# A four-layer graph kernel on one core: layer 1 takes the newest quarter last, mixing puts weighing beside scores, elu is written back into PSUM

## The chip, the cores and the metric

The kernel runs on one core of one Trainium2 chip. The core has five engines that run their own instruction streams and meet by semaphores: TensorE (PE in the profile), VectorE (DVE), ScalarE (ACT), GpSimd (POOL) and SyncE (SP, used here to issue DMAs). TensorE reads its operands from SBUF and writes into PSUM; the others read and write both, GpSimd only SBUF here. The metric is device time in microseconds of one execution, the median of several runs.

## The reference

Four layers, each a layer norm over `x + layer(x)`, with x of shape (8, 2048, 64) and one adjacency matrix of 2048 x 2048. What matters here are layers 0 and 1:

```python
h = x @ W
alpha = softmax(where(H.T > 0, leaky_relu(h @ a_node), NEG))    # per hyperedge e
agg = einsum('ben,bnf->bef', alpha, h)
beta = sigmoid((h @ a_gn)[:, None, :] + (agg @ a_ge)[:, :, None])
all_he = elu(beta[..., None] * h[:, None] + (1 - beta[..., None]) * agg[:, :, None])
industry = einsum('nm,bmf->bnf', adj / deg, x @ W_ind)
coefs1 = softmax(where(H > 0, attn_scores(elu(agg)), NEG))      # attn_scores(f) = tanh(f @ fcW) @ av
g = einsum('bne,benf->bnf', coefs1, all_he)
coefs2 = softmax(attn_scores(stack([industry, g])))             # the mixing: two candidates
out0 = coefs2[0] * industry + coefs2[1] * g
x = layernorm(x + out0)                                         # layer 0
x = layernorm(x + (D^-1/2 (adj + I) D^-1/2) @ x @ W1.T)         # layer 1
```

Layers 2 (a Chebyshev graph convolution with an attention matrix) and 3 (three propagation steps) follow, and the change does not touch them.

## The kernel before

The batch of 8 is taken as four pairs (p = 0 to 3), so that two batches of 64 features fill 128 columns. The 2048 nodes are 16 tiles of 128 (t), or four quarters of 512 (c). The adjacency matrix stays in SBUF. Matmul operands are split by `split` (L167, L168) into a high part, cast on ScalarE, and a low part, so that every product with the adjacency takes two matmuls.

**One stream of filler.** Layer 0's products `adj @ x` (`products`, L383 to L418) and layer 1's (`layer1`, L1012) are a generator. It yields after each matmul, and other stages take from it by `fill(n)` (L420): n matmuls with the adjacency are written between two steps of their own, so TensorE has work while the other engines do theirs. Each matmul also counts a `tick` (L309 to L330): work handed to `after(n, f)` or `later(n, f)` is written n matmuls later. The order of instructions on each engine is thus largely written out in the program; what is wrapped in `tc.keep_in_program_order` (`pin`) keeps its place, and the rest may be moved by a scheduler.

**Hyperedge stage** (`begin`, L746 to L768, and the loop at L774 to L808). A node lies in 1 to 12 hyperedges; nodes are sorted by that count, so the 16 tiles have 12, 5, 5, 4, ... down to 1 slots, 57 in all. Per slot: three matmuls make `pz` in PSUM, eight fills at most are taken; VectorE multiplies `pz` by the ratios `R` (L793), ScalarE takes exp (L795) into `y` in SBUF, VectorE forms elu from both into `y` (L797) and weighs `y` by `co` (L800 for the first slot, L802 for others), and GpSimd adds it to `acc` (L803). After the last slot of a tile an indirect DMA scatters `acc` to `gs_hbm` (L805). `begin` for the next tile is called after the first slot's matmuls: it splits the gathered row `hrow` (low part on GpSimd), makes `ps` and from it, on VectorE, `R` and `co` (L761, L764, L765, L767). `slots` (L281 to L300) transposes the slot numbers into `pslot`, casts them twice on ScalarE (L288) and makes the one-hot matrices of a tile with two ScalarE operations per slot (L299, L300). `pz`, `pslot` and other small tiles share a PSUM pool tag `mm` of three buffers; the fills accumulate in other PSUM tiles. Also in this stage: the degrees of the nodes (`degrees`, L341 to L356) and their inverses (`inverses`, L358 to L381).

**Mixing** (L1050 to L1070), 16 steps i = (pair, quarter). `mix_load` and `mix_g` load the two candidates, `mix_ind` and `mix_g` bring them into one layout (`pi`, `pg`), `mix_scores` (L916 to L926) makes four `pf` matmuls and their tanh, takes differences and adds `gn` to the residual `r`; `mix_weigh` (L935, L937) makes `pd` from the differences, its tanh `th` and from it the weighed candidate `ind`; `mix_end` (L948 to L957) transposes it into `pt`, adds, normalizes (`normalized`, L843 to L867: VectorE, ScalarE's square, GpSimd's power, VectorE) and stores the quarter of x1, after which SP loads the residual of step i + 2. Between the groups, `fill(8)` or `fill(9)`. All these PSUM tiles share a tag `mm` of four buffers.

**Layer 1.** When a quarter of x1 is stored, `l1_parts` (L969, L972) reloads it into one of two staging buffers (`staged`, L204), scales it by `dinv` on GpSimd and splits it. `layer1(p)` runs over two halves g of the columns, and in each over all 16 tiles t (so the quarters 0, 1, 2, 3 in order); then `l1_end` (L991 to L996) multiplies by W1 (`po`), adds `x1` (reloaded by `l1_load`, L981) and normalizes. `load_xn` (L1010) loads the finished 1 MB of a pair on ScalarE's queue.

**End of the mixing.** After the last step the program drains stores by `fill(1)`, loads the node embeddings into `xn` by SP (L1098), takes `fill(32)`, and then for four blocks calls `make_el` (L1107 to L1117; its matmul is `pb`) with `fill(16)` between; after the second, `load_xn` may start. Then the check of the norms, and the remaining fills. Layer 2 begins with `apt_tile` (L1149 to L1156).

Of the kernel before, what the change touches and what calls it, by code (L numbers as in the profile page):

```python
# [56 lines left out]
def tile_gnn_fast(  # L57
# [28 lines left out]
    P = 128  # L86
# [230 lines left out]
    def after(n, f, *more):  # L317

        soon.append([n, lambda: (f(), after(*more) if more else None)])
# [22 lines left out]
    def products():  # L342
# [3 lines left out]
        def degrees(g):  # L346
            du = pph.tile([P, 2, C], F32, tag="ph", name=f"du{g}", bufs=2)
            for t in range(NT):
                for i in range(2):
                    mm(  # L350
                        du[:, i, :], lhsT=ones_r, rhs=adj_c(t, 2 * g + i), start=t == 0, stop=t == NT - 1
                    )
                    yield
            for i in range(2):
                c = 2 * g + i
                r = slice(c * P // NCH, (c + 1) * P // NCH)  # L356
                evacuate(deg4[r, :], du[r, i, :])

        def inverses():

            pdc = places["small"]([P, JT, P], "pdc")
            for j in range(JT):
                transpose(pdc[:, j, :], deg4[:, cols(j, P)])
            pdc = pdc.rearrange("p j (c r) -> p c j r", c=NCH)[:, :, :, 0]
            d1 = deg1.rearrange("p (c j) -> p c j", c=NCH)
            nc.vector.tensor_scalar(d1, pdc, 1.0, None, op0=ALU.add)
            nc.gpsimd.tensor_tensor(dinv, deg1, neg_half[:, :NT], ALU.pow)
            nc.vector.tensor_scalar(d1, pdc, 1.0, None, op0=ALU.max)
            nc.vector.reciprocal(deg1, deg1)
            for _ in range(20):  # L370
                yield
            for c in range(NCH):
                pt = places["small"]([P, C], "pinv")
                for j in range(JT):
                    k = c * JT + j
                    transpose(pt[:, cols(j, P)], deg1[:, k:k + 1].to_broadcast([P, P]))
                row = va.tile([P, C], F32, tag="ut", name="inv", bufs=2)
                nc.scalar.copy(row, pt)
                nc.sync.dma_start(inv_hbm[:, cols(c)], row)
                for _ in range(4):  # L380
                    yield  # L381

        for p in range(NP):  # L383
# [358 lines left out]
    with ExitStack() as pb_scope:  # L742
        pps = pb_scope.enter_context(tc.tile_pool(name="pb_ps", bufs=1, space=PSUM))
        places["small"] = lambda shape, name: pps.tile(shape, F32, tag="mm", name=name, bufs=3)
        pl = pb_scope.enter_context(tc.tile_pool(name="pl", bufs=1))

        def begin(t):

            k = tiles.index(t)
# [11 lines left out]
            nc.vector.tensor_tensor(  # L761
                R[:, 0:S], ps[:, 0:S, 0, :], hrow[:, None, BF:BF + 8].to_broadcast([P, S, B]), ALU.add
            )
            nc.vector.tensor_reduce(R[:, S], ps[:, 0:S, 1, :].rearrange("p s b -> p b s"), AX.X, ALU.add)  # L764
            nc.vector.reciprocal(R[:, 0:S + 1], R[:, 0:S + 1])  # L765
            co = pl.tile([P, 12, B], F32, tag="co", name="co", bufs=2)
            nc.vector.tensor_tensor(  # L767
                co[:, 0:S], ps[:, 0:S, 1, :], R[:, S:S + 1, :].to_broadcast([P, S, B]), ALU.mult  # L768
            )
            return S, both, ohs, R, co  # L770


        tiles = [*range(NT - 2), NT - 1, NT - 2]
        now = begin(0)  # L774
        slots(tiles[1], pps, "mm", 3)
        for k, t in enumerate(tiles):
            S, both, ohs, R, co = now
            acc = pl.tile([P, B, F], F32, tag="acc", name="acc", bufs=2)
            for s in range(S):
                pz = pps.tile([P, C], F32, tag="mm", name="pz", bufs=3)  # L780
# [12 lines left out]
                nc.vector.tensor_tensor(z, z, R[:, s, :, None].to_broadcast([P, B, F]), ALU.mult)  # L793
                y = pl.tile([P, B, F], F32, tag="y", name="y", bufs=3)
                nc.scalar.activation(y, z, AF.Exp, bias=-1.0)  # L795

                nc.vector.scalar_tensor_tensor(y, z, 1.0, y, op0=ALU.max, op1=ALU.min)  # L797
                cb = co[:, s, :, None].to_broadcast([P, B, F])
                if s == 0:
                    nc.vector.tensor_tensor(acc, y, cb, ALU.mult)  # L800
                else:
                    nc.vector.tensor_tensor(y, y, cb, ALU.mult)  # L802
                    nc.gpsimd.tensor_tensor(acc, acc, y, ALU.add)  # L803

            nc.gpsimd.indirect_dma_start(  # L805
                out=gs_hbm[:], out_offset=bass.IndirectOffsetOnAxis(ap=order[:, t:t + 1], axis=0),
                in_=acc.rearrange("p b f -> p (b f)"), in_offset=None,
            )  # L808

    hrp_scope.close()  # L810
    hy_scope.close()
# [94 lines left out]
    def mix_scores(i):  # L906
# [56 lines left out]
    def l1_parts(p, c):  # L963

        if (p, c) not in stored:
            due.add((p, c))
            return
        y = staged("y")
        nc.sync.dma_start(y, x1_hbm[p][:, wide(c), :])  # L969

        def scale():
            pin(nc.gpsimd.tensor_tensor(y, y, dinv[:, wide(c), None].to_broadcast([P, JT, P]), ALU.mult))  # L972

        def cast():
            part[p, c] = split(va, y, f"v{c}", 1, [P, JT, P], pin=True)

        after(16, scale, 6, cast)

    def l1_load(p, c):
        x1 = staged("x1")  # L980
        nc.sync.dma_start(x1, x1_hbm[p][:, wide(c), :])  # L981
        return x1

    def l1_end(p, c, ut, x1):
# [5 lines left out]
        def add_up():  # L990
            pin(nc.vector.tensor_tensor(r, po, dinv[:, wide(c), None].to_broadcast([P, JT, P]), ALU.mult))  # L991
            pin(nc.gpsimd.tensor_tensor(r, r, x1, ALU.add))

        def end():
            if p < NP - 1:
# [2 lines left out]
            load_xn()  # L998

        dst = xn[p][:, wide(c), :] if p == NP - 1 else r  # L1000
        after(4, add_up, 6, *normalized(lp, r, dst, True, end))

    room = []

# [6 lines left out]

    def layer1(p):  # L1012

        for g in range(2):
            own = (2 * g, 2 * g + 1)
            ug = None
            for t in range(NT):
                while (p, t // JT) not in part:
                    yield "wait"
                if ug is None:  # L1020
                    ug = pph.tile([P, 2, C], F32, tag="ph", name="u1", bufs=2)
                    u = {c: ug[:, c % 2, :] for c in own}
                for i in range(2):
                    for c in own:
                        mm(
                            u[c], lhsT=part[p, t // JT][i][:, t % JT, :], rhs=adj_c(t, c),
                            start=t == 0 and i == 0, stop=t == NT - 1 and i == 1,
                        )
                        tick()
                        yield  # L1030
                if g == 1 and p + 1 < NP and t % JT == JT - 1:
                    l1_parts(p + 1, t // JT)
            for k, c in enumerate(own):
                ut = va.tile([P, C], F32, tag="ut", name="ut", bufs=2)
                pin(nc.scalar.copy(ut, u[c]))
# [91 lines left out]
    norms = staged("emb").rearrange("p t f -> p (t f)")[:, 0:NT * D].rearrange("p (t d) -> p t d", d=D)  # L1127
    nc.sync.dma_start(norms, emb.rearrange("(t p) d -> p t d", p=P))
    nc.vector.tensor_tensor(norms, norms, norms, ALU.mult)
    nrm = ap_.tile([P, NT], F32, name="nrm")  # L1130
    nc.vector.tensor_reduce(nrm, norms, AX.X, ALU.add)
    nc.vector.tensor_reduce(wrong[:, 5:6], nrm, AX.X, ALU.max)
    nc.vector.tensor_scalar(wrong[:, 5:6], wrong[:, 5:6], SUM_LIMIT, None, op0=ALU.is_gt)
    for _ in filler:
        pass

# [1486 lines left out]
```

## Time and profile before

| | before |
|---|---|
| runs | 1742.09, 1739.12, 1742.03 us; median 1742.03 |
| profiled execution | 1745.85 us, of which the span is 1743.7 |
| mean granted TensorE clock | 0.984 |
| instructions | 27994 |
| busy in the span: PE, DVE, ACT, POOL | 1660.8 (95%), 832.2 (48%), 589.5 (34%), 571.8 (33%) us |
| hyperedge stage, mixing, end of the mixing | about 63 to 221, 221 to 436, 436 to 523 us |

A group's line in the profile reads: line, engine, operation, output tile <- input tiles, shapes, count, then the busy time in us and the mean of one instruction in ns, and then the idle time of that engine just before the group's instructions with what ended it. A line of the waits reads: engine, what it wanted to do, what it waited for, then us in total, how many times, and the longest. A line of the timeline has the start, the duration, the instruction, and in brackets the engine's idle time before it. In a table by stage, each engine has its busy time and, in brackets, its instructions; PEclk is the granted clock as a share of full speed.

### The profile page before, as it was taken

To read this page: it belongs to the slowest core of one execution; us is meant where nothing else is said; L and a number is where in the kernel's file an instruction comes from. 1 tells how busy PE (TensorE), PEld (TensorE's weight loads), DVE (VectorE), ACT (ScalarE), POOL (GpSimd) and SP (SyncE) were. 2 spreads that over 40 slices of the span, in tenths; PEclk is the share of its full clock that TensorE was granted. 3 is DMA by queue.
4 is the path that set the end of the run, shared out by engine and by line. 5 is a ranking of instruction groups with operands and counts; after the bars stand their busy time and mean duration, and the time that the engine had idled before them with its cause. 6 is when DMAs were issued, how large, how long until landed. Compare 5 with 4: busy or idle time off the path is not lost.

```text
span 1743.7 us, 27994 instructions
## 1 busy us (share of the span) xinstructions
PE 1660.8 (95%) x11196; PEld 1209.8 (69%) x11196; DVE 832.2 (48%) x1547; ACT 589.5 (34%) x1031; POOL 571.8 (33%) x515
## 2 busy tenths in 40 slices
PE   6888899999899999999999999999989999999996
PEld 4667666666674444478788878888767877878775
DVE  7688845778642221210136147777523433433332
ACT  1345533444222212111213267878512222212221
POOL 4578845556534443422023001313210200202001
PEclk9999999999999999999999999999999999999998
DMA  9833334444330000027344457675571121211211
GB/s 342 277 126 124 125 122 136 142 145 146 112 121 6 30 27 5 24 71 293 112 133 138 117 137 154 138 168 123 152 260 43 49 61 43 61 48 42 57 42 39
DMA packets 171180, 195.83 MB, mean 112 GB/s; under 512 B 71536, under 2 KB 116336, under 8 KB 169760
## 3 DMA queue, kind: packets, MB, share of 16 engines
q1 hardware_dynamic: 160096, 154.54, 30.4%
q0 software_dynamic: 8544, 30.68, 5.2%
q10 hardware_dynamic: 2400, 8.72, 1.4%
q8 instruction: 90, 1.47, 0.4%
q14 instruction: 50, 0.41, 0.1%
HBM read 126.72 MB, written 67.17 MB: 111 GB/s over the span
## 4 chain that ended last, share of the span: by engine, by line
PE 78%; DVE 4%; DMA 3%; POOL 2%; issue 2%; ACT 1%; SPq 1%; POOLq 0%; ACTq 0%; DVEq 0%
PE u L172 39%; PE ua L172 13%; PE py L172 8%; PE pw L172 6%; PE ug L172 3%; PE pr L172 2%; PE po L172 1%; PE pf L172 1%; PE pt L175 1%; PE s L172 1%; PE pd L172 1%; PE pi L172 1%; PE pz L172 1%; POOL ln_r L862 0%; DMA adj_more<-adj_hbm 0%
## 5 line engine op out<-in xcount | busy, mean ns | idle before, releaser
L172 PE MATMUL ua<-pt,xn 128*128 128x512 f32 x512 | 230.2, 592 | 1.4 <-DVE pt L1150 1.4
L172 PEld LDWEIGHTS ua<-pt,xn 128*128 128x128 f32 x512 | 96.9, 190 | 111.1 <-issue 104.0
L1514 DVE COPY w_half<-pw 128x512 f32<-128x512 f32 x160 | 109.7, 705 | 91.1 <-PE pw L172 90.2
L1510 ACT COPY w_half<-pw 128x1024 f32<-128x1024 f32 x128 | 130.0, 1015 | 61.6 <-PE pw L172 61.5
L172 PE MATMUL py<-w_half,xg 128*32 128x128 f32 x4096 | 144.2, 281 | 3.2 <-issue 3.2
L172 PE MATMUL u<-adj,v0h 128*128 128x512 f32 x384 | 134.4, 427 | 1.1 <-ACT h L1818 1.1
L172 PEld LDWEIGHTS py<-w_half,xg 128*32 128x32 f32 x4096 | 112.5, 138 | 21.3 <-issue 4.6
L172 PE MATMUL u<-adj_more,v2h 128*128 128x512 f32 x384 | 126.5, 408 | 0.0
L172 PE MATMUL u<-adj_more,v2l 128*128 128x512 f32 x384 | 124.6, 401 | 0.0
L172 PE MATMUL u<-adj,v0l 128*128 128x512 f32 x384 | 124.5, 402 | 0.0
L172 PE MATMUL pw<-est,wst 64*128 64x256 f32 x1024 | 110.8, 320 | 0.8 <-ACT w_half L1510 0.4
L1156 POOL TENSOR_TENSOR acc<-acc,pt 128x512 f32<-128x512 f32 x60 | 76.5, 1276 | 104.2 <-DVE pt L1150 103.5
L1150 DVE TENSOR_SCALAR pt<-pt 128x512 f32<-128x512 f32 x64 | 29.8, 465 | 152.4 <-ACT pt L1149 152.3
L172 PEld LDWEIGHTS pw<-est,wst 64*128 64x128 f32 x1024 | 82.7, 187 | 26.3 <-ACT w_half L1510 16.7
L1727 ACT CAST ar<-fcav 128x512 fp32r<-128x512 f32 x64 | 39.5, 618 | 169.2 <-DMA fcav<-in_adj_t 164.5
L172 PE MATMUL u<-adj_more,v3l 128*128 128x512 f32 x288 | 93.8, 401 | 2.0 <-DVE v3l L168 2.0
L1728 DVE SCALAR_TENSOR_TENSOR ar<-fcav,ar 128x512 f32<-128x512 f32 x64 | 45.2, 707 | 102.9 <-ACT ar L1727 102.9
L172 PE MATMUL u<-adj,v1h 128*128 128x512 f32 x288 | 93.7, 403 | 0.0
L1149 ACT ACTIVATE pt<-s 128x512 f32<-128x512 f32 x64 | 38.0, 598 | 164.4 <-PE s L172 164.4
L172 PE MATMUL u<-adj_more,v3h 128*128 128x512 f32 x288 | 93.6, 403 | 0.0
L1699 POOL TENSOR_TENSOR x<-x,rows 128x512 f32<-128x512 f32 x16 | 22.6, 1433 | 212.0 <-PE pt L175 127.7
L172 PE MATMUL u<-adj,v1l 128*128 128x512 f32 x288 | 92.0, 397 | 0.0
(406 smaller groups left out, 3273.2 us busy)
## 6 DMA issues: line engine op xcount, KB each, us to landing
fcav<-in_adj_t SPq DMA_DIRECT2D x64, 256.0 KB, 2.9
u_hbm<-ut SPq DMA_DIRECT2D x48, 256.0 KB, 2.8
xg<-u_hbm SPq DMA_DIRECT2D x24, 512.0 KB, 7.1
adj<-in_adj_t POOLq DMA_DIRECT2D x16, 512.0 KB, 7.7
adj_more<-in_adj_t POOLq DMA_DIRECT2D x16, 512.0 KB, 7.4
adj_hbm<-adj_more SPq DMA_DIRECT2D x16, 512.0 KB, 6.1
x_hbm<-r SPq DMA_DIRECT2D x28, 256.0 KB, 2.4
hs_hbm<-st ACTq DMA_DIRECT2D x8, 584.0 KB, 5.9
```

The costliest lines, as they stand in the source:

```text
L172: tc.keep_in_program_order(nc.tensor.matmul(*args, **kw))
L175: tc.keep_in_program_order(nc.tensor.transpose(dst, src, ident))
L1149: nc.scalar.activation(pt, s, AF.Exp)
L1150: nc.vector.tensor_scalar(pt, pt, 1.0, None, op0=ALU.max)
L1156: nc.gpsimd.tensor_tensor(accs[c], accs[c], pt, ALU.add)
L1510: pin(nc.scalar.copy(dst, pw.rearrange("p j o n -> p n (j o)")))
L1514: pin(copy(dst[:, :, 2 * j:2 * j + 2], bank.rearrange("p o n -> p n o")))
L1699: nc.gpsimd.tensor_tensor(xs, xs, b2.to_broadcast([P, JT, P]), ALU.add)
L1727: nc.scalar.copy(ar, seen_a)
L1728: nc.vector.scalar_tensor_tensor(ar.bitcast(F32), seen_a, 1.0, ar.bitcast(F32), op0=ALU.mult, op1=ALU.not_equal, accum_out=left[:, t, k:k ...
```

## The change

Four things are changed, all in the order of work or in the place of an operand; no arithmetic is added or left out.

1. Hyperedge stage. Exp is written to `e`; elu is written back over `z` in PSUM, and the weighing reads it from there. The weighing of slot s (`weighed`) is written after the first multiply and the exp of slot s + 1, and the ratios of the next tile after the elu of the first slot. All VectorE operations of the loop are pinned (`hold`).
2. Degrees and inverses: the copies are assigned to fixed engines, the reciprocals come later, and the four inverse rows are spread wider.
3. Mixing: `mix_weigh(i - 1)` stands directly before `mix_scores(i)`; the add of `gn` moves to a function of its own (`mix_sum`) after the next step's `mix_g`; three groups of 11 or 12 fills.
4. Layer 1: for each pair the order of (half, quarters) is (0: 0, 1, 2), (1: 0, 1), (0: 3), (1: 2, 3). The loads into the two staging buffers go through a list (`ask`, `serve`, `left`) that issues one when a buffer is free. At the end, the loads of finished pairs are allowed before `fill(40)`, with `fill(12)` between the four blocks, and the check of the norms is spread.

```diff
@@ degrees, inverses
-                evacuate(deg4[r, :], du[r, i, :])
+                if i:
+                    tc.keep_in_program_order(nc.vector.tensor_copy(deg4[r, :], du[r, i, :]))
+                else:
+                    nc.scalar.copy(deg4[r, :], du[r, i, :])
...
-            for _ in range(20):
+            for _ in range(16):
+                yield
+            kept(nc.vector.tensor_scalar(d1, pdc, 1.0, None, op0=ALU.max))
+            kept(nc.vector.reciprocal(deg1, deg1))
+            for _ in range(4):
                 yield
...
-                for _ in range(4):
+                for _ in range(11):
@@ hyperedge loop
+        def weighed(acc, z, cb, first, t):
+            if first:
+                hold(nc.vector.tensor_tensor(acc, z, cb, ALU.mult))
+            else:
+                y = pl.tile([P, B, F], F32, tag="y", name="y", bufs=3)
+                hold(nc.vector.tensor_tensor(y, z, cb, ALU.mult))
+                nc.gpsimd.tensor_tensor(acc, acc, y, ALU.add)
+            if t is not None:
+                nc.gpsimd.indirect_dma_start(
...
-                nc.vector.tensor_tensor(z, z, R[:, s, :, None].to_broadcast([P, B, F]), ALU.mult)
-                y = pl.tile([P, B, F], F32, tag="y", name="y", bufs=3)
-                nc.scalar.activation(y, z, AF.Exp, bias=-1.0)
-
-                nc.vector.scalar_tensor_tensor(y, z, 1.0, y, op0=ALU.max, op1=ALU.min)
+                hold(nc.vector.tensor_tensor(z, z, R[:, s, :, None].to_broadcast([P, B, F]), ALU.mult))
+                e = pl.tile([P, B, F], F32, tag="y", name="e", bufs=3)
+                nc.scalar.activation(e, z, AF.Exp, bias=-1.0)
+                if rest:
+                    rest.pop()()
+
+                hold(nc.vector.scalar_tensor_tensor(z, z, 1.0, e, op0=ALU.max, op1=ALU.min))
+                if s == 0 and k + 1 < NT:
+                    now[-1]()
                 cb = co[:, s, :, None].to_broadcast([P, B, F])
-                if s == 0:
-                    nc.vector.tensor_tensor(acc, y, cb, ALU.mult)
-                else:
-                    nc.vector.tensor_tensor(y, y, cb, ALU.mult)
-                    nc.gpsimd.tensor_tensor(acc, acc, y, ALU.add)
...
+                rest.append(lambda z=z, acc=acc, cb=cb, s=s, t=t, S=S: weighed(
+                    acc, z, cb, s == 0, t if s == S - 1 else None
+                ))
@@ mixing
+    def mix_sum(i):
         r, gn = rs[i], gns.pop(i)
         after(8, lambda: pin(nc.gpsimd.tensor_tensor(r, r, gn, ALU.add)))
...
-        k = 9 if i > NCH else 8
+        k = 12 if i > NCH else 11
+        if i > 0:
+            mix_weigh(i - 1)
         if i < steps:
             mix_scores(i)
-            fill(k)
-        if i > 0:
-            mix_end(i - 1)
             fill(k)
         if i + 1 < steps:
             mix_load(i + 2)
             mix_ind(i + 1)
             mix_g(i + 1)
-            fill(k)
         if i < steps:
-            mix_weigh(i)
+            mix_sum(i)
+        fill(k)
+        if i > 0:
+            mix_end(i - 1)
             fill(k)
@@ layer 1
-            after(16, scale, 6, cast)
+            after(16, scale, 12, cast)
...
+    def serve():
+        while asked and (taken[0] < 2 or taken[0] - 2 in free_again):
+            taken[0] += 1
+            asked.pop(0)(taken[0] - 1)
...
-        for g in range(2):
+        u, held = {}, [None, None]
+        for g, quarters in ((0, (0, 1, 2)), (1, (0, 1)), (0, (3,)), (1, (2, 3))):
...
-                later(6 + 8 * k, lambda p=p, c=c, ut=ut, x1=l1_load(p, c): l1_end(p, c, ut, x1))
+                    l1_load(p, c)
+                    later(8 + 8 * k, lambda p=p, c=c, ut=ut: l1_end(p, c, ut))
@@ end of the mixing
-    fill(32)
+    room.append(True)
+    load_xn()
+    fill(40)
     for c in range(NCH):
         make_el(c)
-        fill(16)
-        if c == 1:
-
-            room.append(True)
-            load_xn()
+        fill(12)
```

More of the change, by code (lines that the diff above doesn't have):

```diff
@@ L365, in inverses @@
             d1 = deg1.rearrange("p (c j) -> p c j", c=NCH)
-            nc.vector.tensor_scalar(d1, pdc, 1.0, None, op0=ALU.add)
+            kept = tc.keep_in_program_order
+            kept(nc.vector.tensor_scalar(d1, pdc, 1.0, None, op0=ALU.add))
             nc.gpsimd.tensor_tensor(dinv, deg1, neg_half[:, :NT], ALU.pow)
-            nc.vector.tensor_scalar(d1, pdc, 1.0, None, op0=ALU.max)
-            nc.vector.reciprocal(deg1, deg1)
-            for _ in range(20):
+            for _ in range(16):
[3 more added lines that the diff above has]
+            for _ in range(4):
                 yield
@@ L745, in tile_gnn_fast @@
         pl = pb_scope.enter_context(tc.tile_pool(name="pl", bufs=1))
+        hold = tc.keep_in_program_order
         def begin(t):
@@ L760, in begin, with ratios @@
             R = pl.tile([P, 13, B], F32, tag="R", name="R", bufs=2)
[L761 to L765, printed above, removed]
-            co = pl.tile([P, 12, B], F32, tag="co", name="co", bufs=2)
[L767 to L770, printed above, removed]
+            co = pl.tile([P, 12, B], F32, tag="co", name="co", bufs=2)
+            def ratios():
+                hold(nc.vector.tensor_tensor(
+                    R[:, 0:S], ps[:, 0:S, 0, :], hrow[:, None, BF:BF + 8].to_broadcast([P, S, B]), ALU.add
+                ))
+                hold(nc.vector.tensor_reduce(
+                    R[:, S], ps[:, 0:S, 1, :].rearrange("p s b -> p b s"), AX.X, ALU.add
+                ))
+                hold(nc.vector.reciprocal(R[:, 0:S + 1], R[:, 0:S + 1]))
+                hold(nc.vector.tensor_tensor(
+                    co[:, 0:S], ps[:, 0:S, 1, :], R[:, S:S + 1, :].to_broadcast([P, S, B]), ALU.mult
+                ))
+            return S, both, ohs, R, co, ratios
         tiles = [*range(NT - 2), NT - 1, NT - 2]
         now = begin(0)
+        now[-1]()
         slots(tiles[1], pps, "mm", 3)
+        rest = []
+        def weighed(acc, z, cb, first, t):
[7 more added lines that the diff above has]
+                nc.gpsimd.indirect_dma_start(
+                    out=gs_hbm[:], out_offset=bass.IndirectOffsetOnAxis(ap=order[:, t:t + 1], axis=0),
+                    in_=acc.rearrange("p b f -> p (b f)"), in_offset=None,
+                )
         for k, t in enumerate(tiles):
-            S, both, ohs, R, co = now
+            S, both, ohs, R, co, _ = now
             acc = pl.tile([P, B, F], F32, tag="acc", name="acc", bufs=2)
@@ L792, in tile_gnn_fast @@
                 z = pz.rearrange("p (b f) -> p b f", f=F)
-                nc.vector.tensor_tensor(z, z, R[:, s, :, None].to_broadcast([P, B, F]), ALU.mult)
-                y = pl.tile([P, B, F], F32, tag="y", name="y", bufs=3)
-                nc.scalar.activation(y, z, AF.Exp, bias=-1.0)
-                nc.vector.scalar_tensor_tensor(y, z, 1.0, y, op0=ALU.max, op1=ALU.min)
-                cb = co[:, s, :, None].to_broadcast([P, B, F])
-                if s == 0:
-                    nc.vector.tensor_tensor(acc, y, cb, ALU.mult)
-                else:
[L802 to L808, printed above, removed]
+                hold(nc.vector.tensor_tensor(z, z, R[:, s, :, None].to_broadcast([P, B, F]), ALU.mult))
[5 more added lines that the diff above has]
+                if s == 0 and k + 1 < NT:
+                    now[-1]()
+                cb = co[:, s, :, None].to_broadcast([P, B, F])
+                rest.append(lambda z=z, acc=acc, cb=cb, s=s, t=t, S=S: weighed(
+                    acc, z, cb, s == 0, t if s == S - 1 else None
+                ))
+        rest.pop()()
     hrp_scope.close()
@@ L967, in l1_parts, with begin, scale, cast @@
             return
[L968 to L975, printed above, removed]
-        after(16, scale, 6, cast)
-    def l1_load(p, c):
[L980 to L984, printed above, removed]
+        def begin(k):
+            y = staged("y")
+            nc.sync.dma_start(y, x1_hbm[p][:, wide(c), :])
+            def scale():
+                pin(nc.gpsimd.tensor_tensor(y, y, dinv[:, wide(c), None].to_broadcast([P, JT, P]), ALU.mult))
+            def cast():
+                part[p, c] = split(va, y, f"v{c}", 1, [P, JT, P], pin=True)
+                left(k)
+            after(16, scale, 12, cast)
+        ask(begin)
+    asked, taken, free_again = [], [0], set()
+    def ask(f):
+        asked.append(f)
+        serve()
+    def serve():
+        while asked and (taken[0] < 2 or taken[0] - 2 in free_again):
+            taken[0] += 1
+            asked.pop(0)(taken[0] - 1)
+    def left(k):
+        free_again.add(k)
+        serve()
+    x1s = {}
+    def l1_load(p, c):
+        def begin(k):
+            x1 = staged("x1")
+            nc.sync.dma_start(x1, x1_hbm[p][:, wide(c), :])
+            x1s[p, c] = k, x1
+        ask(begin)
+    def l1_end(p, c, ut):
         po = lps.tile([P, JT, P], F32, tag="mm", name="po", bufs=4)
@@ L990, in add_up @@
         def add_up():
+            if (p, c) not in x1s:
+                after(1, add_up)
+                return
+            k, x1 = x1s.pop((p, c))
             pin(nc.vector.tensor_tensor(r, po, dinv[:, wide(c), None].to_broadcast([P, JT, P]), ALU.mult))
             pin(nc.gpsimd.tensor_tensor(r, r, x1, ALU.add))
+            left(k)
+            after(6, *chain)
         def end():
@@ L1000, in l1_end @@
         dst = xn[p][:, wide(c), :] if p == NP - 1 else r
-        after(4, add_up, 6, *normalized(lp, r, dst, True, end))
+        chain = normalized(lp, r, dst, True, end)
+        after(4, add_up)
     room = []
@@ L1012, in layer1 @@
     def layer1(p):
-        for g in range(2):
+        u, held = {}, [None, None]
+        for g, quarters in ((0, (0, 1, 2)), (1, (0, 1)), (0, (3,)), (1, (2, 3))):
             own = (2 * g, 2 * g + 1)
-            ug = None
-            for t in range(NT):
-                while (p, t // JT) not in part:
+            for q in quarters:
+                while (p, q) not in part:
                     yield "wait"
[L1020 to L1035, printed above, removed]
-                later(6 + 8 * k, lambda p=p, c=c, ut=ut, x1=l1_load(p, c): l1_end(p, c, ut, x1))
@@ new lines, in layer1 @@
+                if held[g] is None:
+                    held[g] = pph.tile([P, 2, C], F32, tag="ph", name="u1", bufs=2)
+                    u.update({c: held[g][:, c % 2, :] for c in own})
+                for t in range(q * JT, (q + 1) * JT):
+                    for i in range(2):
+                        for c in own:
+                            mm(
+                                u[c], lhsT=part[p, q][i][:, t % JT, :], rhs=adj_c(t, c),
+                                start=t == 0 and i == 0, stop=t == NT - 1 and i == 1,
+                            )
+                            tick()
+                            yield
@@ L1038, in all_pairs @@
+                if g == 1 and p + 1 < NP and q < 3:
+                    l1_parts(p + 1, q)
+            if 3 in quarters:
+                for k, c in enumerate(own):
+                    ut = va.tile([P, C], F32, tag="ut", name="ut", bufs=2)
+                    pin(nc.scalar.copy(ut, u[c]))
+                    l1_load(p, c)
+                    later(8 + 8 * k, lambda p=p, c=c, ut=ut: l1_end(p, c, ut))
+                if g == 1 and p + 1 < NP:
+                    l1_parts(p + 1, 3)
     def all_pairs():
@@ L1117, in make_el, with bound, largest @@
         nc.sync.dma_start(bias_hbm[:, wide(c), :], bias)
-    fill(32)
+    room.append(True)
+    load_xn()
+    fill(40)
     for c in range(NCH):
         make_el(c)
-        fill(16)
-        if c == 1:
-            room.append(True)
-            load_xn()
-    norms = staged("emb").rearrange("p t f -> p (t f)")[:, 0:NT * D].rearrange("p (t d) -> p t d", d=D)
-    nc.sync.dma_start(norms, emb.rearrange("(t p) d -> p t d", p=P))
-    nc.vector.tensor_tensor(norms, norms, norms, ALU.mult)
-    nrm = ap_.tile([P, NT], F32, name="nrm")
-    nc.vector.tensor_reduce(nrm, norms, AX.X, ALU.add)
-    nc.vector.tensor_reduce(wrong[:, 5:6], nrm, AX.X, ALU.max)
-    nc.vector.tensor_scalar(wrong[:, 5:6], wrong[:, 5:6], SUM_LIMIT, None, op0=ALU.is_gt)
+        fill(12)
+    nrm = ap_.tile([P, NT], F32, name="nrm")
+    def bound(k):
+        norms = staged("emb").rearrange("p t f -> p (t f)")[:, 0:NT * D].rearrange("p (t d) -> p t d", d=D)
+        nc.sync.dma_start(norms, emb.rearrange("(t p) d -> p t d", p=P))
+        def largest():
+            pin(nc.vector.tensor_tensor(norms, norms, norms, ALU.mult))
+            pin(nc.vector.tensor_reduce(nrm, norms, AX.X, ALU.add))
+            pin(nc.vector.tensor_reduce(wrong[:, 5:6], nrm, AX.X, ALU.max))
+            pin(nc.vector.tensor_scalar(wrong[:, 5:6], wrong[:, 5:6], SUM_LIMIT, None, op0=ALU.is_gt))
+            left(k)
+        after(14, largest)
+    ask(bound)
     for _ in filler:
```

## The prediction

> **What bounds the kernel now.** I read the whole first, then the stages, then PE's waits, then the engines that PE waits for. The profiled execution took 1745.85 us: a span of 1743.7 and 2.15 outside it. The median of the runs shown is 1742.03, 3.8 less; I work out a difference on the profiled execution and take it off the median. PE is busy for 1660.8 us of the span, and the diff leaves PE's matmuls as they are: the same `u` and `pz` matmuls, in another order. So the change can win only time in which PE stands still, or runs at half clock. The table by stage, for the hyperedge stage (87 to 221), the mixing (221 to 436) and its end (436 to 523):
>
> ```profile
> core 0: us, PE busy (x) PEld busy (x) DVE busy (x) ACT busy (x) POOL busy (x), PEclk, DMA share, GB/s
> ...
> 87.00:221.00 134.00, 116.82 (x499) 88.81 (x498) 115.24 (x207) 72.51 (x187) 111.21 (x87) 0.96 0.38 123
> 221.00:436.00 215.00, 211.57 (x934) 138.44 (x933) 140.61 (x195) 83.78 (x144) 117.79 (x94) 1.00 0.43 140
> 436.00:523.00 87.00, 76.59 (x342) 56.84 (x341) 48.49 (x85) 22.19 (x41) 38.09 (x27) 0.94 0.37 116
> ```
>
> To be seen: the mixing has 3.4 us without PE, the other two stages 17.2 and 10.4. The gaps of PE's timeline between 82 and 525 sum to 32.0 us: 18.2 in the hyperedge stage (23 gaps), 3.4 in the mixing, 10.4 at its end. Behind long gaps the clock records show half clock: 3.4 us from 129.5, 6.8 from 204.6, 3.4 from 460.6, 6.8 from 481.1. A `u` matmul starts every 0.2325 us at full clock and every 0.425 in such a spell, so each us of it costs about 0.5: 5.1 us in the hyperedge stage, 5.1 at the end of the mixing. PE's waits say on whom:
>
> ```profile
> PE pz L172 <- DVE y L797: 8.2, 12, 1.5
> ...
> PE pb L172 <- DMA xn<-x_hbm: 5.4, 1, 5.4
> ...
> PE pt L175 <- DVE ind L937: 3.8, 2, 3.6
> ...
> PE pz L172 <- ACT slot L288: 2.8, 4, 1.0
> PE pz L172 <- DVE R L764: 2.5, 2, 1.7
> ```
>
> (In us: total, times, longest.) In the hyperedge stage PE waits for a PSUM tile that VectorE has not left. VectorE's groups there (87 to 218) and GpSimd's add:
>
> ```profile
> L802 DVE TENSOR_TENSOR y<-y,co 128x512 f32<-128x512 f32 x34 | 32.9, 989 | 0.2
> L797 DVE SCALAR_TENSOR_TENSOR y<-pz,y 128x512 f32<-128x512 f32 x48 | 31.8, 676 | 4.8 <-ACT y L795 4.5
> L793 DVE TENSOR_TENSOR pz<-pz,R 128x512 f32<-128x512 f32 x47 | 31.7, 686 | 9.6 <-PE pz L172 7.5 <-ACT o L300 1.3 <-ACT y L795 0.7
> L800 DVE TENSOR_TENSOR acc<-y,co 128x512 f32<-128x512 f32 x13 | 13.9, 1066 | 0.0
> ```
>
> ```profile
> L803 POOL TENSOR_TENSOR acc<-acc,y 128x512 f32<-128x512 f32 x34 | 48.6, 1431 | 9.1 <-DVE y L802 7.7 <-DVE R L764 0.6
> ```
>
> The two that read PSUM take 0.68; the two that read two SBUF operands 0.99 and 1.07, though the shortest of them took 0.665. The worst pair took 4.03 us from 167.19, while GpSimd issued an indirect DMA, made `hrl` and added `acc`; PE's 1.45 us gap at 173.68 follows.
>
> **Elu back into PSUM.** The weighing by `co` (L800, L802) now reads z from PSUM and `co` from SBUF. Its nearest row is L793, the same operation on PSUM, at 0.69. So 34 x 0.30 + 13 x 0.38 = 15 us of VectorE's 115 go, and GpSimd's 34 adds may fall from 1.43 to their shortest, 1.27 to 1.30 (5 us). What it adds: a `pz` tile is held until the weighing, which is pinned behind the next slot's first multiply. Per slot VectorE then needs about 3 x 0.62 (start to start) = 1.86 us, PE 8 matmuls x 0.2325 = 1.86; per tile the ratios add 0.84 to VectorE, `ps`, `pslot` and three more fills 1.15 to PE. A tile of two slots: VectorE 4.56, PE 4.87. VectorE fits, barely. I take the waits on it and the one on `inv` (spread by the change) as gone: 8.2 + 2.5 + 1.0 = -11.7.
>
> Against this stands the ring of three PSUM tiles that `pz` shares with `pslot`. In the order of PE's instructions, the `pz` right behind a `pslot` waits for ScalarE's casts of that same `pslot` in 5 of 15 tiles before, and in all 15 after: nothing of PE lies between. The row of such a wait is 2.8 us in 4, so 0.62 to 0.97 each; 10 more at 0.65 are +6.5. Half clock: the spell at 129.5 follows waits that go; of that at 204.6 I count a little: -2 of 5.1. **Sum -7.** Ends: no slot wait beyond the old ones and all half clock gone, -17; half of VectorE's waits stay, ten slot waits at 0.97, +4.
>
> A rule against this edit: the Trainium skill, "VectorE: DVE Perf Modes", section "Rules for kernel authors", says to accept the slow rate on matmul output in PSUM or to copy it to SBUF first if many operations follow. Three operations follow here, and by that rule the change would give VectorE nothing. The rows above say otherwise while GpSimd is busy: 0.68 in PSUM against 0.99. The skill's "SBUF - State Buffer", section "SBUF: two separate sides", has a reason: an operation with two SBUF inputs and a GpSimd one that reads SBUF exclude each other for a whole instruction. L797, with one SBUF input, shows no such delay here.
>
> **Mixing.** Per tile of 512 columns, weighing (`pd`) and the next tile's scores (four `pf`) now stand directly behind each other, and three groups of 11 or 12 fills replace four of 8 or 9. The 3.4 us of gaps may go. New: `pd` and four `pf` need five tiles of a ring of four, so the last `pf` waits for `th`, the tanh of `pd`. That takes 0.59, and PE needs 0.7 for the three `pf` between: no wait if ScalarE is free, up to 0.6 where a square or cast (0.62) lies ahead of `th`. The add of `r` and `gn` moves later on GpSimd; `gn` lands within 5 us and is read some 10 us after its issue, so it hides. Ends -3.4 and 16 x 0.6 = +10; I take **+1**, nearest to the case of a free ScalarE.
>
> **Layer 1's order and the end of the mixing.** A pair's newest quarter is wanted after 80 matmuls instead of 48, 7.4 us later. In the mixing no PE wait shows on these quarters, so it gains there only at the last pair's edges. At the end, before:
>
> ```profile
> 460.20 0.77 PE L175 MATMUL pt<-ident,ind 128*128 128x128 f32 x4 [3.61 <-DVE ind L937]
> ...
> 481.23 1.93 PE L172 MATMUL pb<-bp,xn 16*128 16x64 f32 x8 [5.37 <-DMA xn<-x_hbm]
> ```
>
> Only nine fills lie between the last `pd` and `pt`; SP issues the `emb` loads (L1098) at 474.54, behind store and reload of the last tile, and their data ends the 5.37. These and half clock cost 3.6 + 5.4 + 5.1 = 14.1. After: twelve fills for `pt` (0 to 2 us wait), 40 fills before `pb` (0 to 1). But the two `xn` loads of finished pairs now stand on ScalarE's queue ahead of the cast of the last pair's third quarter, and wait for the last store. That cast's chain from `pt` on: add 0.7, mean and centring 1.4, square 0.6, variance 0.9, power 1.65, scale 0.7, store landing 3, DMA issue 0.7, cast and rest 1.3 = 11 to 13 us, and PE reaches the quarter 6.8 us after `pt`. So a new wait of 5 to 6 us at `u<-v2h`, with 1.7 to 3.4 of half clock. 1 + 5.5 + 2.5 + 0.5 = 9.5 against 14.1: **-4.5**. Ends: no new wait, -13; a longer queue behind the 1 MB loads, +2. The first-come list for the two staging buffers moves SP's loads, with no PE wait on them before. The pinned copies of the degrees and the check of the norms lie beside fills; without that cover they cost one VectorE operation, 0.7 each.
>
> **Sum:** -7 + 1 - 4.5 = -10.5: 1735.4 against the profiled execution, **1731.5** against the median.
>
> **Rivals.** *More goes than I think* (-25, 1717): the casts keep up, since VectorE's freed time lets ScalarE's exp start earlier, and nothing replaces the end's waits. For: PE is at 1.00 clock and full in the mixing. Against: PE's order has nothing behind `pslot`. *It is eaten* (about -1, 1741): slot casts, or GpSimd in two-slot tiles (5.3 to 6.0 us a tile there against PE's 4.87), keep 17 us of gaps, and `v2h` costs what `pt` and `pb` did. *Slower* (+10, 1752): in the mixing the last `pf` waits for `th` in each of 16 iterations; it decides from 0.6 us each, where ScalarE always has a square or cast ahead of `th`: 10 us, with short half-clock spells 5 more, against 11 won elsewhere at half. For: the order on ScalarE has them there. Against: only one such wait of 0.6 before. That elu does not leave SBUF is excluded: the operands are in the diff.
>
> **Numbers.** Forecast (1720 to 1738) 0.50, more 0.15, eaten 0.18, slower 0.17. A change under 0.2% (3.5 us) can't be told from none. Faster 0.66, same 0.17, slower 0.17. The range, 1716 to 1748, leaves out the far ends of the three sums falling together.
>
> **What would show it.** Right: weighing on VectorE at 0.68, "pz <- DVE" nearly gone, "pz <- ACT slot" 8 to 10 us in 15, `u <- v2h` 5 us near 465. Wrong: "pf <- ACT th" above 5 us; gaps of the hyperedge stage above 17 us or below 6; the wait on `xn` still at 5.

## The result and the profile after

The changed kernel takes 1750.85 us (median of 6 runs, 1746.92 to 1752.85) against 1741.62 before: ratio 1.0046, interval 1.0031 to 1.0061. It is slower, by more than the 0.2% that a measurement can tell from no change. The profiled execution took 1748.99 us, its span 1747.2.

The table by stage of the changed kernel, over the stretches that the prediction showed of before:

```profile
core 0: us, PE busy (x) PEld busy (x) DVE busy (x) ACT busy (x) POOL busy (x), PEclk, DMA share, GB/s
...
87.00:221.00 134.00, 116.28 (x502) 87.39 (x502) 104.21 (x204) 75.02 (x192) 103.93 (x89) 0.99 0.41 135
221.00:436.00 215.00, 207.52 (x916) 138.93 (x914) 135.04 (x193) 80.11 (x138) 120.00 (x93) 0.99 0.42 135
436.00:523.00 87.00, 72.62 (x331) 54.53 (x329) 48.19 (x85) 24.38 (x45) 33.55 (x24) 0.92 0.37 127
```

To be seen: in the hyperedge stage VectorE has 11 us less to do and GpSimd 7, and PE has no more done (116.3 against 116.8). In the mixing and its end PE does 4 us less in each: there the time went. PE's waits between 60 and 530 us (what it wanted, what it waited for, total, times, longest):

```profile
PE pz L172 <- ACT slot L288: 7.8, 12, 1.0
PE u L172 <- ACT v2h L167: 6.8, 1, 6.8
PE po L172 <- ACT ut L1098: 6.5, 1, 6.5
PE pz L172 <- DVE acc L794: 4.5, 5, 1.5
PE pz L172 <- DVE y L797: 4.4, 5, 1.4
PE pf L172 <- DVE r L1049: 3.0, 2, 2.1
PE pg L175 <- DMA gn<-gs_hbm: 3.0, 2, 2.7
...
PE pf L172 <- ACT th L964: 1.5, 2, 1.1
```

The two single waits of 6 to 7 us lie at 473 and 490 us, and each stands in a spell of half clock of some 7 us. From the last `pz` to the first `ua` of layer 2, the same PE work takes 303.0 us (220.78 to 523.76) where it took 294.6 (220.27 to 514.83): 8.4 us, about the whole loss. The same 1246 matmuls keep PE busy for 280.4 us there (280.7 before), so the loss is idle time: 22.6 us where it was 13.8. Half clock costs no more than before, since both spells begin while PE still waits. Behind that, and ahead of the hyperedge loop, the kernels are the same; the first `pz` came between 63.4 and 68.9 us in all runs of this study, without order, also in runs that differ only in later stages. From the first `ua` to the end, the profiled execution of the kernel before took 1228.9 us and that of each of the other fifteen kernels 1221.9 to 1224.8, which no edit explains. So spans alone scatter by some us, and the comparisons below go by the ratios.

What is late shows on the engines behind PE. GpSimd's wait for the load of the residual `r` (221 to 530 us), and SyncE's for the store of a finished tile of x1 (60 to 540), before:

```profile
POOL r L926 <- DMA r<-in_x_n: 25.8, 8, 5.4
```

```profile
SPq L948 <- DVE r L865: 24.7, 13, 5.9
```

The same two in the changed kernel:

```profile
POOL r L955 <- DMA r<-in_x_n: 56.4, 11, 9.4
```

```profile
SPq L977 <- DVE r L892: 77.3, 15, 11.1
```

The store waits for the last step of the tile's normalization (L892) on VectorE. VectorE's timeline at such a place:

```profile
454.23 0.69 DVE L168 TENSOR_TENSOR v0l<-y,v0h 128x512 fp32r<-128x512 f32 x1 [3.58 <-ACT v0h L167]
454.84 0.69 DVE L966 SCALAR_TENSOR_TENSOR ind<-th,ind 128x512 f32<-128x512 f32 x1
455.44 1.29 DVE L948 TENSOR_TENSOR t<-t,t 128x512 f32<-128x512 f32 x2
456.65 0.69 DVE L892 TENSOR_TENSOR r<-ln_c,ln_r 128x512 f32<-128x512 f32 x1
```

GpSimd had that tile's `ln_r` ready at 452.4, but the pinned order puts four instructions ahead: the low part of a quarter, the next tile's `ind`, and the two differences. The operands of all four come from ScalarE, which works off `th` and four tanh in a row (450.25 to 453.7), and then the cast `v0h` that the first of the four waits for. The store leaves at 457.36, the load of `r` behind it at 460.12, GpSimd's add of `gn` (L955) waits 9.39 us for it, and what GpSimd has behind that add is late in turn, layer 1's `r + x` among it. ScalarE's square waits for that, and behind the square stand the copies `ut`:

```profile
466.04 0.63 ACT L884 ACTIVATE ln_c<-r 128x512 f32<-128x512 f32 x1 [10.83 <-POOL r L1050]
...
472.19 0.63 ACT L884 ACTIVATE ln_c<-r 128x512 f32<-128x512 f32 x1 [3.99 <-POOL r L1050]
472.73 1.05 ACT L1098 COPY ut<-u 128x512 f32<-128x512 f32 x2
```

PE's `po` waits for these 6.48 us, at 473.34. This chain was read first; the runs test it link by link.

### The profile page after: what moved, and what is told of

It is laid out like the page before. It is cut to its first block, busy times and chain, and to the rows that moved or that the text cites. A ratio compares the mean times of both kernels' runs of the same rounds, so it can differ in the third digit from the quotient of the medians.

```text
span 1747.2 us, 27970 instructions
## 1 busy us (share of the span) xinstructions
PE 1660.1 (95%) x11196; PEld 1212.4 (69%) x11196; DVE 818.2 (47%) x1547; ACT 590.5 (34%) x1031; POOL 567.1 (32%) x515
## 3 DMA queue, kind: packets, MB, share of 16 engines
q8 instruction: 90, 1.47, 0.3%
## 5 line engine op out<-in xcount | busy, mean ns | idle before, releaser
L172 PEld LDWEIGHTS py<-w_half,xg 128*32 128x32 f32 x4096 | 111.1, 138 | 18.5 <-issue 1.8
```

The costliest lines, as they stand in the source:

```text
L172: tc.keep_in_program_order(nc.tensor.matmul(*args, **kw))
```

## The experiments

Medians, with the ratio to the runs of the kernel before in the same call; "us" is that ratio times 1742, less 1742.

| run | median | ratio, 95% interval | us |
|---|---|---|---|
| changed kernel | 1750.85 | 1.0046 (1.0031 to 1.0061) | +8 |
| e1 hyperedge part alone | 1740.32 | 1.0003 (0.9990 to 1.0017) | 0 |
| e2 rotation of the mixing alone | 1764.68 | 1.0135 (1.0115 to 1.0155) | +23.5 |
| e3 layer 1's order and end alone | 1738.02 | 0.9978 (0.9961 to 0.9996) | -4 |
| e4 changed, three buffers for r | 1747.39 | 1.0035 (1.0022 to 1.0048) | +6 |
| e5 changed, differences later | 1744.78 | 1.0009 (0.9993 to 1.0026) | +1.5 |
| e6 e2, differences later | 1758.58 | 1.0080 (1.0059 to 1.0101) | +14 |
| e7 changed, xn loads late | 1749.89 | 1.0044 (1.0029 to 1.0058) | +7.5 |
| e8 changed, slots early | 1744.71 | 1.0003 (0.9988 to 1.0018) | +0.5 |
| e9 changed without the rotation | 1737.45 | 0.9967 (0.9955 to 0.9980) | -6 |
| e10 e9, slots early | 1732.55 | 0.9942 (0.9920 to 0.9963) | -10 |
| e11 e4, e5 and e8 together | 1739.46 | 0.9982 (0.9969 to 0.9995) | -3 |
| e12 e10, more fills ahead of pg | 1737.42 | 0.9965 (0.9953 to 0.9977) | -6 |
| e13 changed, tile's end earlier | 1745.81 | 1.0023 (1.0008 to 1.0037) | +4 |
| e14 e13, slots early | 1741.56 | 0.9988 (0.9975 to 1.0001) | -2 |

**e1, e2, e3: one part alone on the kernel before.** e1 takes the diff's hunks on degrees, inverses and the hyperedge loop; e2 `mix_sum` and the main loop of the mixing; e3 `l1_parts`, `ask`, `l1_end`, `layer1` and the end of the mixing.

> The kernel before with the hyperedge part of the change alone (elu back into PSUM, pinned order, degrees and inverses). Theory: this part is worth a little, since slot casts take the place of VectorE's waits: from the first to the last pz 153.8 us in the changed kernel against 156.5 before, so about -2 to -3 us (1739). The sum of my prediction had -7 (1735) for it. Rival, that this part is the loss: slower than before by 5 or more.

> The kernel before with the mixing's rotation alone (weighing beside scores, the add of gn in a step of its own, 11 or 12 fills). Theory: the loss comes from this part: GpSimd's add r<-r,gn waits for the load of r (over 45 us in all, before 25.8), everything behind it on GpSimd is late, and the time is 4 to 10 us over before (1746 to 1751). Rival, that the order of the quarters and the end of the mixing are the loss: within 2 us of before.

> The kernel before with layer 1's order of quarters, the list for staging buffers and the new end of the mixing alone. Theory: GpSimd's wait for r stays near 26 us, the wait of po for ut (6.5 us) is not there, u waits for v2h some 5 to 7 us, and the time is within 4 us of before (1738 to 1745). Rival, that the two loads of xn ahead of the cast of v2h are the whole loss: 6 to 10 us over before.

e2 is 23.5 us slower where 4 to 10 were expected. So the rotation alone is a loss, and a far larger one than the whole change. PE's waits of e2 between 60 and 530 us:

```profile
PE u L172 <- ACT v3h L167: 9.8, 1, 9.8
...
PE pf L172 <- ACT th L937: 3.6, 2, 2.7
PE u L172 <- ACT v2h L167: 3.5, 1, 3.5
PE pf L172 <- DVE r L993: 3.4, 2, 2.5
```

The quarter that was stored last (`v3h`) is wanted before it is there: 9.8 us. In the changed kernel, where layer 1 takes that quarter last, this wait is gone. The parts alone sum to +20, together they are +8, so the other parts pay for some of the rotation; that it is the order of the quarters is read from this wait, and no run changes the order by itself on top of e2. GpSimd's wait for `r` in e2 is 61.9 us; in e3 it is 13.9. The wait of 5 to 7 us for `v2h` that was expected of e3 is not there.

The hyperedge part alone is worth nothing in the end. Its loop is shorter, by 2.7 us (153.8 from the first to the last `pz`, 156.5 before), but the first load of `gn` does not come earlier by as much: from the last `pz` to its issue it is 14.2 us in e1 and 13.0 before. `pg` waits 2.35 us for `gn` with 3.4 us of half clock behind it, and at the end of the mixing half clock lasts 10.3 us where it lasted 6.9.

**e4: the residual's buffers.**

```diff
-            rs[i] = mp.tile([P, JT, P], F32, tag="r", name="r", bufs=2)
+            rs[i] = mp.tile([P, JT, P], F32, tag="r", name="r", bufs=3)
...
-            mix_x(i + 2)
+            mix_x(i + 3)
```

(and `mix_x(2)` ahead of the loop.)

> The changed kernel with three buffers for the residual r of the mixing in place of two, and its load issued one step earlier (at the store of tile i that of i+3), so that it no longer waits for a store just issued. Theory: GpSimd's wait for r falls from 56 us to under 15, the waits of po for ut (6.5) and of pf for L1049 (3.0) go, and the time falls by 8 to 13 us to 1738 to 1743. Rival, that the loss is the wait for v2h and what lies behind it: GpSimd's wait falls, the time by no more than 3 us (1748 or more).

GpSimd's waits in the mixing and its end, and PE's, with three buffers:

```profile
POOL ln_r L889 <- DVE ln_e L888: 44.6, 16, 8.0
POOL r L1050 <- DVE r L1049: 32.6, 9, 17.3
POOL y L1002 <- DMA y<-x_hbm: 22.3, 3, 9.2
POOL r L1050 <- DMA x<-x_hbm: 11.2, 3, 9.9
```

```profile
PE u L172 <- ACT v2h L167: 6.9, 1, 6.9
PE po L172 <- ACT ut L1098: 6.0, 1, 6.0
PE pf L172 <- DVE r L1049: 5.7, 2, 5.0
```

The wait for the load of `r` is gone, as meant; PE's waits are not, and the time is lower by 2 to 3.5 us with overlapping intervals. That link of my first theory falls: the load of `r` was late, but GpSimd now waits for `y` and `x`. The longest wait for `x`, 9.9 us, is for a load issued at 458.58, behind the reload (458.17) of the tile stored at 454.85. So both come back to the same late store.

**e5 and e6: what stands ahead of the store on VectorE.** One number, in the changed kernel (e5) and in e2 (e6):

```diff
-        after(5, differences)
+        after(10, differences)
```

> The changed kernel with one number changed: the two differences of the scores (L948) are written 10 matmuls after the scores in place of 5, so that the normalization's last step of the tile before (L892), whose store everything waits for, stands ahead of them in VectorE's pinned order and no longer behind four tanh. Theory (the rotation delays the store on VectorE): SyncE's wait of the x1 stores for L892 falls from 77 us to under 45, the wait of po for ut (6.5) falls under 3, and the time falls by 5 to 10 us to 1741 to 1746. Rival (the rotation is late because a tile takes a third of a step longer from its scores to its end, whatever VectorE's order): the waits stay, and the time is within 2 us of 1750.8.

> The same number changed in the kernel before with the mixing's rotation alone (1764.7). Theory: stores leave earlier and the time falls by 8 us or more, to 1757 or less. Rival, that the longer way of a tile is the loss: within 3 us of 1764.7, with u still waiting about 10 us for v3h.

VectorE's timeline in e5 at the same place:

```profile
453.66 0.68 DVE L966 SCALAR_TENSOR_TENSOR ind<-th,ind 128x512 f32<-128x512 f32 x1
454.26 0.69 DVE L892 TENSOR_TENSOR r<-ln_c,ln_r 128x512 f32<-128x512 f32 x1
454.86 1.29 DVE L948 TENSOR_TENSOR t<-t,t 128x512 f32<-128x512 f32 x2
```

L892 now stands ahead of the differences, and the store leaves 232.9 us after the last `pz` in place of 236.6. The time falls by 6 us in both kernels, in the ratio by 6.4 and 9.6, each uncertain by 4 to 5. The theory holds in size; the waits it named fell less than expected (SyncE 77 to 69 us, `po` 6.5 to 4.8), and in e6 `v3h` still costs 9.5. One reason can be read: `v0l` still stands ahead of L892, and VectorE waits 4.16 us for its `v0h`, which ScalarE casts behind the same four tanh. No run moves that cast. So the place of the differences is worth about half of the 13.8 us that the rotation costs in the changed kernel (e9, below), and the rest is not explained by it.

**e7: the loads of xn.** `room.append(True)` and `load_xn()` back behind the second `make_el`.

> The changed kernel with the loads of the finished pairs (xn) put back behind the second block at the end of the mixing, so that they no longer stand ahead of the cast of v2h on ScalarE. By the step of my prediction the wait of u for v2h (6.8 us) is theirs: it goes, and the time falls by 4 to 8 us. Theory now: GpSimd ended the scaling of that quarter only 0.2 us after the loads were issued, so the wait falls by less than 1 us and the time stays within 2 us of 1750.8.

The wait for `v2h` is 6.2 us in place of 6.8, the time the same. The loads on ScalarE made no more than 0.6 us of that wait.

**e8: the slot numbers.** `slots(...)` in the hyperedge loop ahead of `fill(5)` in place of behind it.

> The changed kernel with the transposition of the slot numbers (pslot) placed five matmuls ahead of the next pz in place of directly ahead of it. Theory: the waits of pz for the slot casts (7.8 us, 12 times) go, VectorE's waits (4.5 and 4.4) stay or grow by 1 to 2, and the hyperedge loop shortens by 5 to 7 us; the time falls by 3 to 7 us, unless the mixing behind it waits longer for gn. Rival, that VectorE bounds the loop: the slot casts' waits reappear as waits for VectorE and the time stays within 2 us.

The casts' waits go, the loop takes 149.1 us where it took 153.8, and the ratio falls by 7.5 us, uncertain by 4; 4.7 of them show in the loop. VectorE's two waits stay (4.0 and 3.7). The matmuls beside `pslot` had been the missing cover.

**e9 and e10: the rotation undone.** e9 is the changed kernel with the mixing's hunks left out, e10 has the early slots too.

> The changed kernel with the mixing's rotation alone undone (hyperedge part, layer 1's order, list and new end kept). Theory (the rotation is the whole loss, the other parts add up): 0 of the hyperedge part and -4 of the order on the kernel before, so 1736 to 1740 and 10 to 14 us under the changed kernel; SyncE's wait of the x1 stores for the normalization back to 24 to 33 us, po's wait for ut under 1. Rival (the parts disturb each other): 1744 or more.

> As the run without the rotation, and the transposition of the slot numbers five matmuls ahead of the next pz. Theory: 4 to 6 us less than without it (it gave 6 in the changed kernel), 1731 to 1735, faster than both kernels. Rival (behind a shorter loop the mixing only waits longer for gn): within 2 us of the run without the rotation.

PE's waits of e10, the largest:

```profile
PE pz L172 <- DVE acc L794: 4.0, 6, 1.3
PE pz L172 <- DVE y L797: 4.0, 5, 1.4
PE pb L172 <- DMA xn<-in_emb: 3.1, 1, 3.1
PE pg L175 <- DMA gn<-gs_hbm: 2.5, 1, 2.5
```

In e9 SyncE waits 33.0 us for L892, `po` 0.5, and `v2h` is not waited for at all. VectorE's timeline of e9 at the place shown above has L892 ahead of the differences, waiting for GpSimd's `ln_r` alone:

```profile
443.82 1.52 DVE L892 TENSOR_TENSOR r<-ln_c,ln_r 128x512 f32<-128x512 f32 x1 [1.16 <-POOL ln_r L889]
...
450.13 2.38 DVE L948 TENSOR_TENSOR t<-t,t 128x512 f32<-128x512 f32 x2 [3.87 <-ACT t L943]
```

Undoing the rotation is worth 13 to 14 us, uncertain by 3 to 4, as expected, and with e2 it shows that the rotation is the loss. The early slots are worth 4 to 5 us more, and e10 is faster than both kernels: 0.9942 (0.9920 to 0.9963).

**e11: the mends together.**

> The changed kernel with all three mends of its parts: differences written 10 matmuls after the scores, three buffers for the residual r, slot numbers transposed early. If their gains (6, 3.5 and 6) add up: 1735 to 1737. If the first two mend the same delay: 1739 to 1742. The rotation's own longer way stays, so it should not go below the run without the rotation that has the early slots.

1739.5: the three gains do not add up, and the time is in the range that was expected if the two mends of the late store mend the same delay. Whether it is these two, or one of them and the slots, that overlap, no run shows. `v2h` (6.9) and `po` (3.9) are still waited for.

**e12: matmuls moved ahead.** `fill(28)` ahead of the first `mix_g` becomes `fill(44)` in e10.

> As the run without the rotation and with early slots, with 44 fills in place of 28 ahead of the first pg of the mixing. Theory (the hyperedge part's gain is given back where pg waits for the first gn): pg's wait of 2.4 us and the half clock behind it (1.6) go, 2 to 4 us less than the run with 28. Rival (16 matmuls fewer are left for the end): the waits of u for the quarters at the end grow by as much, within 1.5 us.

The wait for `gn` goes, and a wait of 9.3 us for `v2h` comes in at the end, with 10.3 us of half clock: slower than e10 by 4 to 5 us, where the theory had a gain and the rival no change. The rival's mechanism came, at a higher price: the matmuls that cover the end are the ones that were spent.

**e13 and e14: the tile's end earlier.** Weighing and scores stay side by side:

```diff
-        if i < steps:
-            mix_sum(i)
-        fill(k)
         if i > 0:
             mix_end(i - 1)
             fill(k)
+        if i + 1 < steps:
+            mix_load(i + 2)
+            mix_ind(i + 1)
+            mix_g(i + 1)
+        if i < steps:
+            mix_sum(i)
+            fill(k)
```

(the group of `mix_load`, `mix_ind` and `mix_g` leaves its place ahead of `mix_end`.)

> The changed kernel with weighing and scores still side by side, but with the end of a tile (mix_end) one group of 11 or 12 matmuls after them, ahead of the next tile's loads, in place of two groups. Theory (the loss of the rotation is the longer way of a tile to its store, with VectorE's order a part of it): the x1 stores leave about 2.7 us earlier and ahead of the differences, the waits of po for ut (6.5) and u for v2h (6.8) fall under 3 together, and the time falls to 1736 to 1741, as without the rotation. Rival (weighing and scores side by side cost by themselves, through ScalarE's five tanh in a row and the four PSUM buffers): 1744 or more, with pf waiting for th or L1049 over 4.

> The same with the slot numbers transposed early. Theory: 4 to 6 us less than without, 1731 to 1736, level with the run without the rotation (1732.6). Rival: 1738 or more.

PE's waits and SyncE's in e13:

```profile
PE pb L172 <- issue: 8.4, 1, 8.4
...
PE pt L175 <- DVE ind L966: 5.4, 3, 3.3
```

```profile
SPq L977 <- DVE r L892: 26.9, 12, 6.0
```

The stores wait nearly as little as before (26.9 us), and the waits for `ut` and `v2h` are gone, as the theory had it; but only 4 us of the 13 came back. Other waits took their place: `pt` follows `pd` by one group of matmuls and waits 5.4 us for `ind`, and `pb` waits 8.4 us, with 13.7 us of half clock. The embeddings that it needs are issued on SyncE from 483.9 on, behind the last stores, and land some 6 us after their issue. The time is the rival's (1744 or more) without the rival's sign: `pf` does not wait for `th`, and 1.6 us for L1049. e14 is 1741.6, the rival's too: the early slots give 4 us more, but it does not come level with e10. So an early end of the tile removes the waits that the late store had made. It does not tell the longer way from VectorE's order, since e13 also puts L892 ahead of the differences. What each link is worth by itself can't be given: mended one by one, the next takes over.

## Why the prediction was wrong

- **What bounds the kernel** was right. PE is busy for 1660.1 us (1660.8), and the loss is idle time.
- **Elu in PSUM: the prices were right.** The group lines of VectorE in the changed hyperedge stage:

```profile
L828 DVE SCALAR_TENSOR_TENSOR pz<-pz,e 128x512 f32<-128x512 f32 x47 | 32.8, 698 | 19.2 <-ACT e L824 17.1
L822 DVE TENSOR_TENSOR pz<-pz,R 128x512 f32<-128x512 f32 x47 | 32.5, 690 | 3.2 <-PE pz L172 2.2 <-ACT o L300 1.0
L797 DVE TENSOR_TENSOR y<-pz,co 128x512 f32<-128x512 f32 x35 | 24.1, 687 | 6.4 <-POOL acc L798 6.0
L794 DVE TENSOR_TENSOR acc<-pz,co 128x512 f32<-128x512 f32 x13 | 8.8, 680 | 0.0
```

  Weighing from PSUM takes 0.69 and 0.68, as forecast, and GpSimd's add 1.294. So the advice to copy matmul output to SBUF if many operations follow (the Trainium skill, "VectorE: DVE Perf Modes", "Rules for kernel authors") would have misled here: with GpSimd busy, the weighing took 0.99 and 1.07 us from SBUF, and 0.69 and 0.68 from PSUM. The slot casts' waits came as forecast too (7.8 us in 12; I had 8 to 10 in 15).
- **That VectorE's waits go, was wrong.** 10.7 us were to vanish; 8.9 stayed. Elu waits 17.1 us for exp, in 16 waits; in 13 of them, 15.7 us, that exp starts on ScalarE right behind a cast or a one-hot operation. ScalarE's timeline at one of them, with the exp of a tile's first slot last:

```profile
115.19 0.53 ACT L288 CAST slot<-pslot 64x128 bf16<-64x128 f32 x2 [1.63 <-PE pslot L175]
115.76 0.69 ACT L299 ACTIVATE far<-slot,number 128x128 bf16<-128x128 bf16 x2
116.36 0.49 ACT L300 ACTIVATE o<-far 128x128 fp32r<-128x128 bf16 x2
116.75 0.68 ACT L299 ACTIVATE far<-slot,number 128x128 bf16<-128x128 bf16 x2
117.34 0.49 ACT L300 ACTIVATE o<-far 128x128 fp32r<-128x128 bf16 x2
117.74 0.58 ACT L824 ACTIVATE e<-pz 128x512 f32<-128x512 f32 x1
```

  I had counted VectorE's busy time per slot and not whom it waits for. That the late exp is what keeps PE waiting is read from these lines; no run moves the one-hot operations. From the first to the last `pz`, PE's idle time fell by 0.8 us (18.2 for 19.1), where I had 5; what the loop won beyond that, 1.8, is less half clock. So the loop won 2.7 us for my 7, and the wait for `gn` and half clock behind it took them (e1: 0).
- **The mixing is the step that failed.** "I take +1, nearest to the case of a free ScalarE." I priced the rotation by the PSUM ring alone, `pf` waiting for `th`: that came to 1.5 us. I did not follow what the two groups written side by side put ahead of the tile in flight on VectorE: L892 behind two differences that need four tanh, and behind a low part whose cast stands behind the same tanh. Nor did I count that a tile has 55 to 60 matmuls from its scores to its end where it had 40 to 45, nor ask of the residual `r` what I asked of `gn`. The step is +23.5 alone and +13 to +14 in the changed kernel, so it makes some 13 of the 18.5 us between forecast (-10.5) and result (+8), and the hyperedge part 7. How the 13 divide stays open: the place of the differences gave back about 6, the earlier end of a tile about 4, and the later add of `gn` (`mix_sum`) was not run by itself.
- **Layer 1's order and the end** came out at -4 (e3), as summed, but not by the way I gave. In e3 there is no wait for `v2h`, and `pb` still waits 3.1 us where I had at most 1; in the changed kernel it is 6.8 us, near my 5 to 6, and not because of the `xn` loads (e7). That quarter's load was issued only at 479.71: SyncE waited 3.0 us for its store (473.07) to land and 3.1 for GpSimd's `r + x` (L1050), and GpSimd scaled the quarter at 487.61. And the part whose gain I had seen "only at the last pair's edges" keeps 10 to 12 us of the rotation's loss away (+8 for a sum of +20; +13.8 for +23.5), most likely by the last quarter's later use.
- **The rivals.** The slower one gave 1752, close to the measured time, by a mechanism that did not happen: its sign of "`pf <- ACT th` above 5 us" is absent. A right number there is no hit.

## What to carry to other kernels

When two groups of work are moved next to each other, list for each in-order engine what now stands ahead of the step that frees a buffer or starts a store, and what each of these waits for; a busy-time count per step does not show it. Two edits can hide each other: try each part alone, since a good one can pay for a bad one. Work that covers waits is a stock: matmuls spent on one gap are missing at the next.

## What the runs showed of the hardware

In the changed kernel the casts made PE wait 0.62 us eleven times and 1.03 once between 88 and 215 us, and none of these waits had half clock at it. The one spell there, 3.4 us from 128.8, starts at the end of a wait of 1.40 us that had others of 1.47, 0.84 and 0.48 in the 7.5 us ahead of it. Waits of 2.35 to 2.69 us (`pg` for `gn`; e1 and the changed kernel) had 3.4 us of half clock at their end, the waits of 6.48 and 6.80 us 6.9, and that of 8.43 us in e13 13.7; these longer spells began 2.8 to 6.3 us before the wait ended. The length of the wait alone does not decide it: one of 2.08 us at 406.43 in the changed kernel had none, and one of 1.80 us at 418.49 in e9 had 3.4.

VectorE's operations from PSUM kept 0.68 to 0.70 us beside a busy GpSimd, and GpSimd's add fell from 1.43 to 1.29 us when VectorE's two-operand reads of SBUF were gone. In e1, which changes the hyperedge part alone, it is 1.29; in e2 and e3, which leave that part as it was, 1.43.
